# Order of weight loads, row gathers and a GpSimd power in the second layer's sorted expert tiles

## Chip, cores and metric

One core of a Trainium2 chip. The metric is the device time of one execution in microseconds; three runs of the kernel before gave 946.13, 953.25 and 954.22 (median 953.25). All arithmetic is fp32.

## The reference, cut to what matters

Two layers over 16 sequences of 112 tokens (1792 tokens of 256 values), each a gated cross-attention to 375 context rows and then a gated mixture of experts. The change sits in the second layer's experts:

```python
h_norm = layer_norm(h, rn_g, rn_b)
g = softmax(einsum('bsd,ed->bse', h_norm, router_w))        # 4 experts
top2_w, top2_idx = top_k(g, 2); top2_w /= sum(top2_w) + 1e-8
hid = relu(layer_norm(einsum('bsd,edh->bseh', h, w1), ln_g, ln_b))   # 256 -> 512
expert_out = einsum('bseh,ehd->bsed', hid, w2)                       # 512 -> 256
out = sum(expert_out[top2_idx] * top2_w)
return layer_norm(out, on_g, on_b)
```

## The kernel before

**Stages.** The first layer's attention and routed experts take up to 583 us; the rest of its experts follows, then the second layer's attention (its score matmuls run from 645 to 733 us). From 740 us on the second layer's experts run as 39 *units*, one in each step of the loop of L1519 (its index is j; unit j starts in step j). A unit is 128 rows through one expert:

- units 0 to 7: token tiles 0 and 1, each through all four experts ("dense");
- units 8 to 30: 23 *sorted tiles* (unit 8 + t is tile t). The middle ten token tiles are routed: each token goes to its two best experts only. Its two copies are gathered into tiles of 128 rows of one expert, with room for the worst case;
- units 31 to 38: token tiles 12 and 13, dense again. They keep TensorE busy while the tiles' results are gathered back.

**A unit's work**, spread over three steps: `unit_hidden` (L1323) multiplies by w1 into PSUM `ph` (4 matmuls, L1327) and takes the mean and variance on VectorE; `unit_normed` (L1337) makes the normed rows; one step later `unit_turn` (L1352) transposes them (`ptz`, L1356), and ScalarE applies scale, bias and relu (L1360); two steps later `unit_out` (L1366) multiplies by w2 into `py` (8 matmuls, L1371). A sorted tile's result is scaled on VectorE into `yr` (L1376) and stored to DRAM `yg1` by SyncE (L1377). A sorted tile's rows are transposed by `unit_in` (L1315, `px`, L1319) two steps before its unit.

**What feeds it.** The order of every engine's instructions in this part is the order of the program text (a manual schedule); each engine and the DMA-issuing queue of SyncE go through theirs in order. Three streams matter:

- *Weights.* `weights_in` (L1279) loads an expert's 1028 KB into one of six buffers, issued by SyncE (L1288; before it SyncE reads the expert's number into a register, L1284). Called at the end of step j for units up to j+3. The buffer that unit u takes was last read by unit u-6, whose last matmul is in step u-4. The store of unit u-5 is emitted earlier in the same step, so it stands ahead of the load of u in SyncE's queue.
- *Rows.* `rows_for` (L1303) issues a gather of 128 KB by GpSimd (L1307) into one of four buffers, at the end of step j for units up to j+4. A buffer is free again after the `px` of the unit four before.
- *Routing.* `routing()` (L1403) is a generator that is advanced by `go_on`, so many parts at a step as `counts` (L1506) says. It yields `taker` (L413), the list of rows that each tile gathers, and `of_rows` (L417).

**The later dense gates.** `dense_gates(R0 + NR, True)` (L1389) computes token tiles 12's and 13's weights in parts, advanced by `next(gating)` at L1541. It calls `gates_of`, whose VectorE differences (L270, L271) feed a power on GpSimd (L273) in place of an exponential on ScalarE. The results are read first in step 33.

**The end.** After the last tile's store, GpSimd gathers each routed token's two results (`fetch1`, L1454, 20 gathers), and `end_one` (L1447) adds, norms and stores a token tile. The number of `end_one` calls per step is listed at L1556. Every `fetch1` waits for all stores to `yg1`.

```python
            attended(n)
            beside(n, 1)
            go_on(counts.get(j, (0, 0))[1])
            if ahead + 4 <= j < stored:
                next(gating, None)
                if j % 3 == 0:
                    end_one()
            # then weights_in for units j+1 .. j+3, rows_for for units j+1 .. j+4
```

Here `ahead` is 8 and `stored` is 32.

Of the kernel before, what the change touches and what calls it, by code (L numbers as in the profile page):

```python
# [56 lines left out]
def tile_flamingo(  # L57
# [11 lines left out]
    def bc(ap, shape):  # L69
        return ap.unsqueeze(len(ap.shape)).to_broadcast(shape)  # L70
# [125 lines left out]
    def stats_of(mv, i, src):  # L196
        st = work.tile([P, 6], F32, tag="bnst", name="bnst")
        nc.vector.bn_stats(st, src)  # L198
        nc.vector.bn_aggr(mv[:, i, :], st)  # L199
# [62 lines left out]
    def gates_of(wk, lg, tops, e, nt, tiny, scale, powers=False):  # L262


        sh = [P, nt, e]
        n = nt * e
        both = wk.tile([P, n + nt], F32, tag=f"g{e}_{nt}", name="g", bufs=1)
        total = wk.tile([P, nt], F32, tag=f"gs{e}_{nt}", name="gs", bufs=1)
        g, second = both[:, :n].rearrange("p (i e) -> p i e", e=e), both[:, n:]
        nc.vector.tensor_tensor(g, lg, bc(tops[0], sh), ALU.subtract)  # L270
        nc.vector.tensor_sub(second, tops[1], tops[0])  # L271
        if powers:
            nc.gpsimd.tensor_tensor(both, euler.to_broadcast([P, n + nt]), both, ALU.pow)  # L273
        else:
            nc.scalar.activation(both, both, AF.Exp)
        yield
        nc.vector.tensor_reduce(total, g, AX.X, ALU.add)
        nc.vector.scalar_tensor_tensor(total, total, tiny, second, ALU.mult, ALU.add)
        nc.vector.tensor_scalar(total, total, 1.0, None, ALU.add)
        nc.vector.reciprocal(total, total)  # L280
        if scale is not None:
            nc.vector.tensor_scalar(total, total, scale, None, ALU.mult)
        gates = keep.tile([P, nt, 2], F32, tag=f"gates{e}_{nt}", name="gates")
        nc.vector.tensor_copy(gates[:, :, 0], total)
        nc.vector.tensor_mul(gates[:, :, 1], second, total)
        return gates
# [211 lines left out]
    with tc.tile_pool(name="a0", bufs=2) as a0, tc.tile_pool(  # L498
# [314 lines left out]
        def beside(n, where):  # L813
            place.update(at=where, n=0)
            for f, args in side.get((n, where), ()):
                f(*args)
# [22 lines left out]
    with tc.tile_pool(name="f0", bufs=3) as f0, tc.tile_pool(  # L839
# [69 lines left out]
        units = [(e, t0, w) for t0, w in blocks for e in range(ES)]  # L909
# [16 lines left out]
        at_i, owner_i, taker = (found[name] for name in ("at", "owner", "taker"))  # L926
# [23 lines left out]
    with tc.tile_pool(name="a1", bufs=2) as a1, tc.tile_pool(  # L950
# [315 lines left out]
        units = [(e, i) for e in range(E1) for i in dense_tiles[:R0]]  # L1266
        ahead = len(units)
        units += [(None, t) for t in range(TILES1)]
        units += [(e, i) for i in dense_tiles[R0:] for e in range(E1)]
        weights, loads = {}, []  # L1270

        def key_of(u):

            return ("t", u[1]) if u[0] is None else (units.index(u) < ahead, u[0])

        loads = [key_of(units[0]), key_of(units[R0])]
        routed = {}

        def weights_in(key):  # L1279
            w = wpool.tile([P, WR1], F32, tag="w", name="wr1_sb")  # L1280
            weights[key] = w
            kind, e = key
            if kind == "t":
                e = nc.values_load(  # L1284
                    routed["owner"][0:1, e : e + 1], engines=[mybir.EngineType.SP],
                    min_val=0, max_val=E1 - 1,
                )
                nc.sync.dma_start(out=w, in_=wr1[bass.ds(e, 1)].rearrange("o p w -> p (o w)"))  # L1288
            else:
                nc.sync.dma_start(out=w, in_=wr1[e])  # L1290
# [12 lines left out]
        def rows_for(u):  # L1303
            if u[0] is None and u not in asked:
                asked.add(u)
                g = ctx_pool.tile([P, KD, S], F32, tag="ctx", name="xg1_sb")[:, 0, :D]
                nc.gpsimd.indirect_dma_start(  # L1307
                    out=g, out_offset=None, in_=xn1_rows,
                    in_offset=bass.IndirectOffsetOnAxis(
                        ap=routed["taker"][:, u[1] : u[1] + 1], axis=0  # L1310
                    ),
                )
                rows_in[u] = g
# [9 lines left out]
        def unit_hidden(u):  # L1323
            w, x_u = weights[key_of(u)], xgs.pop(u) if u[0] is None else xrs[u[1]]
            ph = ps_mm.tile([P, HID], F32, tag="mm", name="ph1")
            for k in range(KD):
                nc.tensor.matmul(  # L1327
                    ph, x_u[:, k, :], w[:, k * HID : (k + 1) * HID],
                    start=(k == 0), stop=(k == KD - 1),
                )  # L1330
            mvh = f1.tile([P, 1, 2], F32, tag="mvh", name="mvh", bufs=4)
            stats_of(mvh, 0, ph)
            r = f1.tile([P, 2], F32, tag="rh", name="rh", bufs=4)
            nc.scalar.activation(r[:, 0:1], mvh[:, 0, 1:2], AF.Sqrt, bias=eps)
            hs[u] = ph, mvh, r
# [67 lines left out]
        def routing():  # L1403
            lg = lg1[:, R0 : R0 + NR, :]
            ohs, tops = yield from two_largest(f1, lg, E1, NR)
            parts = places(f1, ps_t, "t", ohs, E1, TILES1, NR)
            next(parts)
            yield
            gating = gates_of(f1, lg, tops, E1, NR, 1e-8, None)
            next(gating)  # L1410
            next(parts)
            yield
            routed["owner"] = next(parts)
            yield
            routed["at"] = at_once(parts)
            yield
            gates = at_once(gating)
            routed["taker"], routed["rows"] = yield from takers(
                f1, ps_t, "t", routed["at"], E1, TILES1, NR, gates,

                lambda: keep.tile([P, KD, N], F32, tag="oT", name="tables").rearrange(
                    "p k n -> p (k n)"
                ),
            )
# [50 lines left out]
        def attend(n):  # L1475
            if n < B:
                ps[n] = scores1(n)
            if n + 2 < B:
                context(n + 2)
                context_rows(n + 2)  # L1480
            if n == B - 2:
                for key in loads:
                    weights_in(key)
            if 0 <= n - 2 < B:
                apply1(n - 2, pTs.pop(n - 2))
            if n % G in (1, 2) and (n // G + 1) * G < B:
                queries1((n // G + 1) * G, n % G - 1)

        def attended(n):
            if n < B:  # L1490
                ps[n] = divided(*ps[n])
            if 0 <= n - 1 < B:
                pTs[n - 1] = turn1(ps.pop(n - 1))
# [9 lines left out]


        parts, gating = routing(), dense_gates(R0 + NR, True)
        counts = {1: (0, 2), 2: (1, 1), 3: (1, 2), 4: (1, 1), 5: (1, 1), 6: (1, 99)}  # L1506
        stored = ahead + TILES1 + 1
        fetches = [(R0, 0), (R0 + 1, 0)]
        for i in range(R0, R0 + NR):
# [5 lines left out]
        def go_on(k):  # L1515
            for _ in range(k):
                next(parts, None)

        for j in range(steps):  # L1519
            n = B + j  # L1520
            attend(n)
            if j < len(units):
                unit_hidden(units[j])
            beside(n, 0)
            if 0 <= j - 1 < len(units):
                unit_turn(units[j - 1])
            go_on(counts.get(j, (0, 0))[0])
            if j < len(units):
                unit_normed(units[j])
            if j >= ahead - 1:  # L1530
                first = j + 2 if j >= ahead else j + 1
                for u in units[first : j + 3]:
                    if u[0] is None:
                        unit_in(u)
            if 0 <= j - 2:
                unit_out(units[j - 2])
            attended(n)
            beside(n, 1)
            go_on(counts.get(j, (0, 0))[1])
            if ahead + 4 <= j < stored:  # L1540
                next(gating, None)  # L1541
                if j % 3 == 0:
                    end_one()

            for k in range(j + 1, min(j + 4, len(units))):
                if key_of(units[k]) not in weights and (units[k][0] is not None or "owner" in routed):
                    weights_in(key_of(units[k]))
            for k in range(j + 1, min(j + 5, len(units))):
                if "taker" in routed:
                    rows_for(units[k])  # L1550
            if j >= stored:
                for i, r in [fetches.pop(0) for _ in range(min(5 if j == stored else 4, len(fetches)))]:
                    fetch1(i, r)
                    if r:
                        to_end.append((i, ys[i, 0]))
                for _ in range((0, 0, 1, 1, 1, 2, 2, 2, 2)[j - stored]):  # L1556
                    end_one()
        while to_end or ending:
            end_one()
# [110 lines left out]
```

## Time and profile before

| what | us |
|---|---|
| runs | 946.13, 953.25, 954.22; median 953.25 |
| the profiled execution's own time | 950.83 |
| its span, first to last instruction | 949.1 |
| TensorE busy over the span | 880.1 (93%) |
| units 8 to 30, first `ph` of unit 8 to first `ph` of unit 31 | 791.15 to 897.21 = 106.06 |
| of that, TensorE busy | 98.94 |
| after the last sorted tile's store (908.6 to the end) | 40.4, TensorE busy 24.55 |

A profile line of the timeline reads: start, duration, engine, source line, operation, output<-inputs, shape, count, and in brackets the idle time before it with what ended it. SPq is SyncE's queue of DMA issues.

### The profile page before, as it was taken

Reading aid. Unit: us, or ns where it says so; the run is one execution under the profiler, and the core shown is the slowest. Engines: PE = TensorE matmul, PEld = TensorE weight load, DVE = VectorE, ACT = ScalarE, POOL = GpSimd, SP = SyncE. Lnnn points to the kernel's source line nnn. Section 1 sums busy time; section 2 is a strip of 40 time slices with the busy share of each in tenths; the row PEclk is TensorE's granted clock in tenths of the full one; section 3 lists DMA queues with packets and bytes.
Section 4 is the critical chain, followed back from the end, with each engine's and each line's share of the span. In section 5 each row is a group of like instructions: output and inputs, shape, how many; then the busy total and the mean of one; then the engine's idle time right before and its main releaser. Section 6 shows DMA issues by size and latency. Waiting matters only on the chain.

```text
span 949.1 us, 18431 instructions
## 1 busy us (share of the span) xinstructions
PE 880.1 (93%) x7168; PEld 637.6 (67%) x7168; DVE 473.4 (50%) x1253; ACT 349.8 (37%) x856; POOL 236.1 (25%) x439
## 2 busy tenths in 40 slices
PE   6899999999999979999999999989999898889994
PEld 3566666666666546789888887667778675656662
DVE  3666666565666435122222222675555554654557
ACT  3455555556555413101111110224222453444453
POOL 3231221110111120112222212771334303211054
PEclk9999999999999999799999999999999999999998
DMA  7300100010010001329999995422445243887844
GB/s 254 122 3 1 45 24 23 24 39 25 23 40 14 7 12 56 144 81 325 322 309 320 320 314 158 136 61 82 122 134 187 101 179 100 278 293 248 300 134 116
DMA packets 42871, 129.93 MB, mean 137 GB/s; under 512 B 5872, under 2 KB 22384, under 8 KB 33568
## 3 DMA queue, kind: packets, MB, share of 16 engines
q1 hardware_dynamic: 36384, 113.54, 35.6%
q0 software_dynamic: 5856, 14.69, 5.5%
q8 instruction: 56, 0.92, 0.4%
q10 hardware_dynamic: 544, 0.52, 0.2%
q14 instruction: 31, 0.25, 0.1%
HBM read 115.36 MB, written 13.37 MB: 136 GB/s over the span
## 4 chain that ended last, share of the span: by engine, by line
PE 73%; DMA 12%; DVE 7%; POOL 4%; issue 2%; ACT 2%; SPq 0%; DVEq 0%; POOLq 0%; ACTq 0%
DMA wr_sb<-in_wr_dram 10%; PE pt L638 6%; PE pt L657 6%; PE py L1371 5%; PE pt L537 5%; PE ph L1327 5%; PE sp L610 5%; PE phr L872 4%; PE ph L472 4%; PE pyr L884 4%; PE sp L550 3%; PE po L1170 3%; PE py L482 2%; PE ps L1121 2%; PE pa L1159 2%
## 5 line engine op out<-in xcount | busy, mean ns | idle before, releaser
L617 DVE TENSOR_REDUCE mz<-sp 112x2 f32<-112x750 f32 x128 | 114.2, 935 | 56.2 <-PE sp L610 56.2
L645 ACT ACTIVATE pT<-pt 125x336 f32<-125x336 f32 x256 | 94.7, 456 | 65.0 <-PE pt L638 65.0
L872 PE MATMUL phr<-xgT,wr_sb 128*128 128x128 f32 x656 | 82.9, 280 | 9.5 <-DVE xgT L862 9.2
L206 POOL TENSOR_SCALAR rstd<-mv 128x1 f32<-128x1 f32 (+1 forms) x49 | 12.4, 252 | 300.6 <-DVE mv L199 294.8
L872 PEld LDWEIGHTS phr<-xgT,wr_sb 128*128 128x128 f32 x656 | 77.2, 192 | 14.1 <-DVE xgT L862 13.9
L853 POOL DMA_INDIRECT xg_sb<-xn_rows,taker x41 | 39.1, 953 | 170.6 <-PE px L860 124.3
L877 ACT ACTIVATE hTr<-phr 128x512 f32<-128x512 f32 x41 | 24.5, 597 | 154.4 <-PE phr L872 154.4
L862 DVE TENSOR_SCALAR xgT<-px,wr_sb 128x128 f32<-128x128 f32 x82 | 24.9, 346 | 109.7 <-DMA wr_sb<-in_wr_dram 101.3
L884 PE MATMUL pyr<-wr_sb,hTr 128*128 128x256 f32 x328 | 77.4, 380 | 0.0
L1371 PE MATMUL py<-wr_sb,hT 128*128 128x256 f32 x312 | 77.4, 394 | 0.0
L657 PEld LDWEIGHTS pt<-pT,va 125*32 125x32 f32 x1536 | 38.0, 109 | 39.1 <-ACT pT L645 33.6
L884 PEld LDWEIGHTS pyr<-wr_sb,hTr 128*128 128x128 f32 x328 | 59.4, 191 | 6.3
L1371 PEld LDWEIGHTS py<-wr_sb,hT 128*128 128x128 f32 x312 | 58.4, 197 | 6.7
L638 PE MATMUL pt<-qm,kt 32*125 32x112 f32 x1536 | 61.2, 283 | 0.7 <-ACT kt L542 0.3
L657 PE MATMUL pt<-pT,va 125*32 125x112 f32 x1536 | 58.7, 264 | 2.0 <-ACT pT L645 2.0
L638 PEld LDWEIGHTS pt<-qm,kt 32*125 32x125 f32 x1536 | 49.1, 183 | 15.8 <-issue 11.7
L1360 ACT ACTIVATE hT<-ptz,wr_sb 128x128 f32<-128x128 f32 x156 | 57.9, 449 | 0.0
L610 PE MATMUL sp<-kt,qt 32*112 32x375 f32 x512 | 56.6, 494 | 1.2 <-ACT qt L569 0.8
L537 PE MATMUL pt<-ctx_sb,wk 128*128 128x375 f32 x128 | 51.6, 527 | 5.8 <-DMA ctx_sb<-in_ctxT_dram 5.8
L198 DVE BATCH_NORM_STATS2 bnst<-ph 128x6 f32<-128x512 f32 x39 | 27.2, 696 | 46.9 <-PE ph L1327 46.8
L1327 PE MATMUL ph<-wr_sb,xgT 128*128 128x512 f32 x92 | 46.3, 628 | 4.5 <-DMA wr_sb<-in_wr_dram 4.5
L542 ACT ACTIVATE kt<-pt,bks,spots 128x375 f32<-128x375 f32 x64 | 39.0, 659 | 22.7 <-PE pt L537 22.6
(273 smaller groups left out, 1520.3 us busy)
## 6 DMA issues: line engine op xcount, KB each, us to landing
wr_sb<-in_wr_dram SPq DMA_DIRECT2D x41, 1025.0 KB
wr_sb<-in_wr_dram SPq DMA_DIRECT2D x31, 1028.0 KB, 5.3
ctx_sb<-in_ctxT_dram SPq DMA_DIRECT2D x32, 375.0 KB, 5.7
yg<-yr SPq DMA_DIRECT2D x64, 128.0 KB, 6.7
ctxn_sb<-in_ctxN_dram SPq DMA_DIRECT2D x16, 375.0 KB
xn_rows<-xn SPq DMA_DIRECT2D x24, 128.0 KB, 2.5
out_dram<-yb SPq DMA_DIRECT2D x10, 128.0 KB, 1.7
w_sb<-in_w1s_dram SPq DMA_DIRECT2D x2, 512.0 KB
```

The lines of the kernel that those rows point to most:

```text
L537: nc.tensor.matmul(pk, wk0_sb[:, k, c * P : (c + 1) * P], ctxs[b][:, k, :], start=(k == 0), stop=(k == KD - 1),)
L610: nc.tensor.matmul(sps[j // 2][:TQ, j % 2, :S], qt[r : r + HP, c, t0 : t0 + TQ], kt[r : r + HP, g, u, :], start=True, stop=True,)
L617: nc.vector.tensor_reduce(mz[:, 2 * h : 2 * h + 2, HD * (1 - u)], sp[:TQ, :, :S], AX.X, ALU.max, negate=True,)
L638: nc.tensor.matmul(sts[j][:SC, s * TQ : (s + 1) * TQ], kt[r : r + HP, c // 2, c % 2, s * SC : (s + 1) * SC], qm[r : r + HP, :], start=True ...
L645: nc.scalar.activation(pT[:, j, :], sts[j][:SC, : NSC * TQ], AF.Exp)
L657: nc.tensor.matmul(po[r : r + HP, :], va[:, s, (c // 2) * 8 + j * 2 + c % 2, :], pT[:, j, s * TQ : (s + 1) * TQ], start=(s == 0), stop=(s ...
L853: nc.gpsimd.indirect_dma_start(out=g, out_offset=None, in_=xn_rows, in_offset=bass.IndirectOffsetOnAxis(ap=taker[:, t : t + 1], axis=0),)
L872: nc.tensor.matmul(ph[:, m, :], a[:, k, m * P : (m + 1) * P], xgT[:, k, :], start=(k == 0), stop=(k == KD - 1),)
L884: nc.tensor.matmul(py, hT[:, m, :], c[:, m, :], start=(m == 0), stop=(m == KH - 1))
L1327: nc.tensor.matmul(ph, x_u[:, k, :], w[:, k * HID : (k + 1) * HID], start=(k == 0), stop=(k == KD - 1),)
L1360: nc.scalar.activation(hT[:, m, :], pt[:, m, :], AF.Relu, bias=w[:, c + KH + m : c + KH + m + 1], scale=w[:, c + m : c + m + 1],)
L1371: nc.tensor.matmul(py, hT[:, m, :], w[:, c : c + D], start=(m == 0), stop=(m == KH - 1))
```

## The change

Four edits, all in the unit loop and in `gates_of`:

1. `weights_in` for units j+1 to j+3 is called after `unit_hidden` instead of at the end of the step: in SyncE's queue a load now stands ahead of the same step's store to `yg1`.
2. `rows_for` is called in the middle of the step, and for units up to j+5.
3. The last parts of `routing()` run in step 6 ahead of `unit_normed` (two parts there, none at the end of the step).
4. The dense gates' generator gets one more stop, between the differences and the power, and is advanced at j = 12, 13, 17 and 20 only; `end_one` takes the other multiples of 3 (15 to 30). In the last steps one `end_one` more is called at j = 36.

```diff
@@ gates_of
         nc.vector.tensor_sub(second, tops[1], tops[0])
         if powers:
+            yield
             nc.gpsimd.tensor_tensor(both, euler.to_broadcast([P, n + nt]), both, ALU.pow)
@@ the unit loop
-        counts = {1: (0, 2), 2: (1, 1), 3: (1, 2), 4: (1, 1), 5: (1, 1), 6: (1, 99)}
+        counts = {1: (0, 2), 2: (1, 1), 3: (1, 2), 4: (1, 1), 5: (1, 1), 6: (2, 0)}
...
             if j < len(units):
                 unit_hidden(units[j])
+
+            for u in units[j + 1 : j + 4]:
+                if key_of(u) not in weights and (u[0] is not None or "owner" in routed):
+                    weights_in(key_of(u))
             beside(n, 0)
             if 0 <= j - 1 < len(units):
                 unit_turn(units[j - 1])
             go_on(counts.get(j, (0, 0))[0])
+
+            if "taker" in routed:
+                for u in units[j + 1 : j + 6]:
+                    rows_for(u)
...
             if ahead + 4 <= j < stored:
-                next(gating, None)
-                if j % 3 == 0:
+
+                if j - ahead in (4, 5, 9, 12):
+                    next(gating, None)
+                elif j % 3 == 0:
                     end_one()
-
-            for k in range(j + 1, min(j + 4, len(units))):
-                if key_of(units[k]) not in weights and (units[k][0] is not None or "owner" in routed):
-                    weights_in(key_of(units[k]))
-            for k in range(j + 1, min(j + 5, len(units))):
-                if "taker" in routed:
-                    rows_for(units[k])
...
-                for _ in range((0, 0, 1, 1, 1, 2, 2, 2, 2)[j - stored]):
+                for _ in range((0, 0, 1, 1, 2, 2, 2, 2, 2)[j - stored]):
                     end_one()
```

Every engine gets the same instructions as before. TensorE's and ScalarE's are in the same order, but for three `end_one` square roots on ScalarE; SyncE's, GpSimd's and VectorE's change places as told.

## Prediction

> **What bounds the kernel now.** I read the page first: TensorE is busy 93% of the span, and the chain of work that ended last is 73% TensorE and 12% DMA. So time is lost where TensorE waits for DMA. The waits from 690 us on, where the changed loop runs, say which ones. Columns: who waited for whom, us in total, times, longest.
>
> ```profile
> POOL g L273 <- DVE g L271: 14.6, 1, 14.6
> ...
> PE px L1319 <- DMA xg_sb<-xn_rows,taker: 5.7, 3, 2.7
> ...
> PE ph L1327 <- DMA wr_sb<-in_wr_dram: 4.5, 2, 3.4
> ```
>
> TensorE waits three times for gathered rows and twice for weights. The first line is no loss by itself, but GpSimd is an in-order engine: what stands behind its power (L273) waits too. GpSimd's timeline:
>
> ```profile
> 783.53 1.09 POOL L1307 DMA_INDIRECT xg_sb<-xn_rows,taker  x1 [13.88 <-DVE of_rows L417]
> ...
> 802.90 0.94 POOL L1307 DMA_INDIRECT xg_sb<-xn_rows,taker  x1 [3.16 <-PE px L1319]
> 818.43 1.99 POOL L273 TENSOR_TENSOR g<-euler,g 128x10 f32<-128x10 f32 x1 [14.59 <-DVE g L271]
> 820.61 1.03 POOL L1307 DMA_INDIRECT xg_sb<-xn_rows,taker  x1 [0.19 <-issue]
> ```
>
> No gather is issued between 802.90 and 820.61, although one is due in every step. Next TensorE's timeline, the first `ph` matmuls of units 20, 21, 24 and 25:
>
> ```profile
> 845.64 1.88 PE L1327 MATMUL ph<-wr_sb,xgT 128*128 128x512 f32 x4
> ...
> 853.31 3.07 PE L1327 MATMUL ph<-wr_sb,xgT 128*128 128x512 f32 x4 [3.40 <-DMA wr_sb<-in_wr_dram]
> ...
> 867.40 1.88 PE L1327 MATMUL ph<-wr_sb,xgT 128*128 128x512 f32 x4
> 872.72 1.99 PE L1327 MATMUL ph<-wr_sb,xgT 128*128 128x512 f32 x4 [1.05 <-DMA wr_sb<-in_wr_dram]
> ```
>
> An undisturbed step is 4.10 us (`ph` at 837.44, 841.54, 845.64). The chain at unit 21 tells how late its load was:
>
> ```profile
> 844.40 8.87 DMA wr_sb<-in_wr_dram
> 853.26 0.04 issue
> 853.31 3.07 PE ph L1327 x4
> ```
>
> SyncE's queue tells why it began only at 844.40:
>
> ```profile
> 839.32 0.34 SPq L1288 DMA_DIRECT2D wr_sb<-in_wr_dram  x1
> 842.25 0.32 SPq L1377 DMA_DIRECT2D yg<-yr  x1
> 843.23 0.34 SPq L1445 DMA_DIRECT2D out_dram<-wv  x1
> 844.40 0.34 SPq L1288 DMA_DIRECT2D wr_sb<-in_wr_dram  x1
> ```
>
> The load of unit 21 stands behind the store of unit 16, which waits for that unit's `py` and VectorE. Its own buffer was free one step earlier. Last the stretches (length, busy of each engine, granted TensorE clock, DMA share, GB/s):
>
> ```profile
> 820.00:832.00 12.00, 9.34 (x34) 6.02 (x33) 6.85 (x23) 3.66 (x12) 5.23 (x6) 0.86 0.78 263
> 832.00:853.30 21.30, 17.91 (x79) 12.48 (x78) 11.82 (x27) 9.74 (x30) 4.72 (x5) 1.00 0.90 301
> 853.30:861.00 7.70, 7.69 (x23) 4.69 (x24) 2.34 (x5) 1.95 (x6) 0.94 (x1) 0.78 0.52 204
> ```
>
> After a stall the clock is 0.86 or 0.78: the `ph` group at 853.31 takes 3.07 us where others take 1.88. A stall costs its idle time and a slow stretch after it. The DMA engines are at 0.90 between stalls.
>
> **The change part by part.** TensorE's order does not change, so each stall can be costed by how late the next `ph` is against 4.10 us per step.
>
> *Routing's last parts earlier.* `taker` and `of_rows` are copied at 783.08 because they stand behind `wv` (L1383, 782.68), which waits for `py`. Their input, the `pn` matmuls, ends at 780.84. Moved ahead of the reciprocal they can run at about 780.9 (VectorE is done with the variance at 780.53), so the first gather starts some 2.3 us sooner. Before, TensorE waited 1.68 us for tile 0's rows and 1.33 us for tile 1's. The first landing (2.81 us after issue) then precedes TensorE's arrival at 784.80; the second gather, 1.4 us behind, lands at about 785.8 where TensorE arrives at 785.2: 0.6 us is left. The whole place costs: `ph` of unit 7 at 782.47 to unit 8 at 791.15 = 8.68, against 1.72+0.44+0.82+1.73 = 4.71 of work (two `px`), so 3.97; the next step 795.99-791.15 = 4.84, so 0.74; together 4.71. Saved: 4.71-0.6 = 4.1. What is pushed back is unit 6's reciprocal, 0.3 us; its reader on ScalarE starts only at 782.20, behind four relus, so this is free; uncovered it would cost 0.3.
>
> *Rows five ahead.* A gather is released by the `px` four units before, whatever its place in the text; only its place against the power counts. 0 by itself.
>
> *The power four units later.* It goes behind 15 gathers instead of 9. Its differences are still made in step 13, so at its new place (step 17) it waits for nothing; it takes 1.99 us between two gathers 4.10 us apart (0.94 busy, some 0.5 between instructions), which leaves about 0.7 us of cover. Uncovered it delays one gather by at most 2 us out of some 16 us of lead. Removed is the stall at 825.57 (2.66 idle): `ph` 820.60 to 828.30 = 7.70, to 833.34 = 5.04, so 3.60+0.94 = 4.54 saved. The gates are read in step 33, made in step 20.
>
> *Loads ahead of stores.* A load now follows the store of the step before, so from unit 14 on each is issued one step, 4.10 us, sooner. SyncE's register read before it (L1284) moves along. The load waits for a buffer whose last reader ended in step u-4, and the store behind it waits for a later `py` (step u-3): the store is not held up in the queue, but its bytes follow the load's. `yr` has four buffers, so 16 us of cover. With transfers as before, the two late loads (by 3.40 and 1.05) come 0.7 and 3 us early. Saved: at unit 21 (853.31-845.64)-4.10 = 3.57 and (859.20-853.31)-4.10 = 1.79; at unit 25 872.72-867.40-4.10 = 1.22 and 876.92-872.72-4.10 = 0.10. Together 6.7.
>
> *What comes after.* Without pauses the DMA engines get no time to catch up. A step needs 1028+128+128 KB = 1.315 MB; at the 301 GB/s of 832 to 853.3 that is 4.37 us, 0.27 more than the step. The load of unit 14 gets 816.49-806.08 = 10.4 us in place of 6.3; alone a load lands in 5.3 (median), so 5.1 us is spare; twelve steps with gathers eat 12×0.27 = 3.2 and leave 1.9. But one landing took 8.87, 3.6 over the median: I expect one or two short stalls, 2.0 us with their slow clock. Bounds: 0 (at 383 GB/s, the best slice of this region, a step takes 3.43) and 8 (at the 282 GB/s of 844 to 848: 4.66, twelve steps eat 6.7 of 5.1, and jitter with slow clock is on top).
>
> Two rules of the skill bear on this. First, "DMA: Bandwidth & Descriptors", section Specifications, gives some 358 GB/s of HBM per core: 3.67 us per step, the cover never shrinks, and the leftover stall would be 0. The row (301 at a share of 0.90, gathers and stores among the loads) says otherwise; I take the row, as it speaks against the change. Second, "TensorE: Matmul & The Clock Gate", section on HAM oscillation, sees the half clock after idle gaps of over about 3.4 us. By it only the stall of 3.40 costs more than its idle time, and the stalls before units 8 and 16 would save 2.4 and 2.7 instead of 4.1 and 4.5, 3.5 us less in all. The trace has a slow stretch after gaps of 1.68+1.33 and 2.66 as well (clock 0.86 over 820 to 832); I take the trace.
>
> *The end.* The fetches wait for the last store to `yg1`: issued at 905.69, landed 2.89 later, behind a load issued at 902.22. Other 128 KB stores land in 1.7. That load goes out a step sooner, so about 1.2 us is saved; 20 gathers, which GpSimd issues back to back, follow it. One more `end_one` at step 36 moves some 2 us of VectorE's work from after the last unit to before it. VectorE is nearly full from 926 to 946, so the sum stays: 0 (between -1 and +1.5).
>
> **The sum.** 4.1+4.5+6.7+1.2-2.0 = 14.5. The profiled execution took 950.83 (span 949.1): 936.3. The median of the runs shown is 2.4 above it: 938.7; I say 938.5.
>
> **The rivals.**
>
> *DMA-bound tiles (0.18).* The loads start sooner but do not end sooner, because the engines are full: at 4.66 us per step the late stalls come back, 6 to 10 us with slow clock. For it: shares of 0.9, landings of 7.5 and 8.87. Against it: after 878, without gathers, 302 GB/s carried steps of 3.9 us with no wait. Time: 943 to 948.
>
> *The end takes it back (0.07).* If the moved `end_one` meets a gather not yet landed, VectorE stalls in front of units 37 and 38 and each step slips by 2 to 3 us, and the first gather still comes late: 947 to 953. Against it: the gather concerned lands at 925.4, and its `end_one` would run at 925.4 at the earliest.
>
> *Slower (0.04).* One mechanism: continuous loads, stores and gathers slow each other, so that a step's bytes need over 5.25 us. From the load of unit 14 (about 804) to that of unit 30 before (its `ph` at 893.33) are 17 loads, 89 us: 5.25 each is break-even, 250 GB/s. At 5.6 the time is about 958. The slowest stretch between stalls was 282.
>
> *It doesn't do what it says (in the 0.07).* If a load were held by something other than the store, its issue would stay: against it, each load follows its store by 1.2 to 2.7 us, register read and an output's store between them.
>
> **How the numbers follow.** The likeliest, 938.5, has 0.71 and its own range 933 to 943. The range that should hold 8 in 10: low 931 (no leftover stall, end 1 us better, a run of the kind of 946), high 947 (most of the DMA-bound case). About 1% is what a measurement of this kernel can tell from no change. Under 943.7 lie the likeliest nearly whole and some of the DMA-bound case: 0.78; slower 0.04; the rest, 0.18, within 1%.
>
> **What would show it.** Right: first gather at about 781; no gather gap of over 5 us at 803 to 820; the power with hardly a wait behind the fifteenth gather; a load directly ahead of each tile's store; `ph` of unit 8 to 31 in about 95 us instead of 106.06. Wrong: `ph` waiting for `wr_sb` more than 3 us in all, landings growing beyond 10 us, or a longer stretch after the last tile's store than 40.4.

## The result, and the profile after

The changed kernel takes 943.62 us in the median of 22 runs (931.75 to 959.58), the kernel before 952.06 beside it (22 runs, 945.02 to 965.77). The ratio of the two is 0.9892, 95% interval 0.9864 to 0.992. That is 10.3 us less, somewhere between 7.6 and 12.9; foretold were 14.5, and 938.5 us. Some executions of either kernel run at a lower TensorE clock and take longer; the medians contain them, the ratio leaves them out. The profiled execution took 942.06 (span 940.4) against 950.83.

Cut at the first `ph` of a unit, the profiled executions compare as follows. The two columns on the right are runs told of below: the kernel before in a second trace, and the version that was found to be best.

| us | before | after | before_again | px_tail_back |
|---|---|---|---|---|
| start of unit 0 | 739.67 | 738.61 | 735.05 | 740.40 |
| unit 0 to 7 | 42.80 | 42.81 | 42.80 | 42.81 |
| unit 7 to 9 (first rows, routing) | 13.51 | 13.40 | 11.75 | 9.81 |
| unit 9 to 31 (sorted tiles) | 101.22 | 89.78 | 99.96 | 89.78 |
| unit 31 to the end | 51.91 | 55.76 | 54.74 | 50.74 |
| span | 949.1 | 940.4 | 944.3 | 933.5 |

Before against after: 1.06 come from ahead of the change and are chance (unit 0 starts between 735 and 744 whatever the kernel, in all traces but one), 0.1 from the place of the routing, 11.4 from the sorted tiles, and 3.9 are given back at the end. The tiles did what was foretold and more, the routing did nothing, and the end went the other way. Each has its own reason.

First TensorE's waits of the changed kernel from 690 us on (who waited for whom, us in total, times, longest):

```profile
PE ptz L1357 <- ACT hT L1350: 5.4, 2, 3.8
PE px L1320 <- ACT hT L1350: 3.1, 1, 3.1
...
PE ptz L1357 <- ACT hT L1361: 1.4, 1, 1.4
```

The lines that ended in DMA (`xg_sb` 5.7, `wr_sb` 4.5) are gone. But `px` waits 3.1 us for ScalarE, and `ptz` more than the 4.8 us of before: these are the routing and the end.

GpSimd's timeline (start, duration, instruction, idle time before it):

```profile
780.29 1.09 POOL L1308 DMA_INDIRECT xg_sb<-xn_rows,taker  x1 [11.69 <-DVE rh L1340]
...
826.33 0.95 POOL L1308 DMA_INDIRECT xg_sb<-xn_rows,taker  x1 [3.15 <-DVE bnst L198]
827.30 2.00 POOL L274 TENSOR_TENSOR g<-euler,g 128x10 f32<-128x10 f32 x1
830.45 1.03 POOL L1308 DMA_INDIRECT xg_sb<-xn_rows,taker  x1 [1.14 <-PE px L1320]
```

The first gather starts at 780.29 (before 783.53), and the power stands between two gathers without a wait of its own; before it had waited 14.59 us. The gather behind it is delayed by nothing that matters: idle time of 1.14 is left.

SyncE's queue around the load of unit 21, the one that was 3.40 us late:

```profile
829.51 0.33 SPq L1289 DMA_DIRECT2D wr_sb<-in_wr_dram  x1
832.44 0.33 SPq L1378 DMA_DIRECT2D yg<-yr  x1
833.61 0.33 SPq L1289 DMA_DIRECT2D wr_sb<-in_wr_dram  x1
```

and the `ph` of units 20 and 21 on TensorE:

```profile
839.93 1.88 PE L1328 MATMUL ph<-wr_sb,xgT 128*128 128x512 f32 x4
...
844.03 1.88 PE L1328 MATMUL ph<-wr_sb,xgT 128*128 128x512 f32 x4
```

The load of unit 21 is the one at 833.61: 6.3 us ahead of unit 20's `ph`, where it was 1.2 ahead (844.40 to 845.64). The last recorded signal of its landing is at 841.26, so 2.8 us are to spare, and unit 21 follows unit 20 after 4.10. A load still starts 1.2 us behind a store, but behind that of the step before.

Last the stretches (length, busy of PE, PEld, DVE, ACT, POOL, granted clock, DMA share, GB/s):

```profile
820.00:832.00 12.00, 12.00 (x55) 8.52 (x54) 7.23 (x18) 5.84 (x19) 4.92 (x4) 1.00 0.93 322
832.00:853.30 21.30, 21.30 (x93) 14.82 (x92) 15.39 (x43) 10.47 (x33) 4.73 (x5) 1.00 0.94 324
```

TensorE is busy without a gap at full clock, and the DMA engines carry 322 to 324 GB/s where they had carried 263 and 301. A step's 1.315 MB in 4.10 us is 321 GB/s: the engines keep up exactly.

### The profile page after: what moved, and what is told of

It is laid out like the page before. It is cut to its first block, busy times and chain, and to the rows that moved or that the text cites. A ratio compares the mean times of both kernels' runs of the same rounds, so it can differ in the third digit from the quotient of the medians.

```text
span 940.4 us, 18431 instructions
## 1 busy us (share of the span) xinstructions
PE 878.8 (93%) x7168; PEld 638.0 (68%) x7168; DVE 473.9 (50%) x1253; ACT 349.9 (37%) x856; POOL 235.9 (25%) x439
## 4 chain that ended last, share of the span: by engine, by line
PE 79%; DMA 7%; DVE 6%; POOL 3%; issue 2%; ACT 2%; another core or an unknown queue 0%; DVEq 0%; ACTq 0%; POOLq 0%
DMA wr_sb<-in_wr_dram 7%; PE py L1372 7%; PE ph L1328 6%; PE pt L639 6%; PE pt L658 6%; PE phr L873 5%; PE pt L538 5%; PE sp L611 5%; PE pyr L885 5%; PE ph L473 4%; PE sp L551 3%; PE po L1171 3%; PE py L483 2%; PE ps L1122 2%; PE pa L1160 2%
## 5 line engine op out<-in xcount | busy, mean ns | idle before, releaser
L639 PEld LDWEIGHTS pt<-qm,kt 32*125 32x125 f32 x1536 | 49.1, 183 | 15.7 <-issue 11.7
L473 PE MATMUL ph<-xT,w_sb 128*128 128x512 f32 (+1 forms) x112 | 46.4, 563 | 0.6 <-DVE x_sb L487 0.6
```

The costliest lines, as they stand in the source:

```text
L473: nc.tensor.matmul(ph, a[:, k, m * P : (m + 1) * P], xT[:, k, t0 * P : (t0 + n) * P], start=(k == 0), stop=(k == KD - 1),)
L639: nc.tensor.matmul(sts[j][:SC, s * TQ : (s + 1) * TQ], kt[r : r + HP, c // 2, c % 2, s * SC : (s + 1) * SC], qm[r : r + HP, :], start=True ...
```

## The experiments

Edits are against the changed kernel unless the text says otherwise. Ratios are to the kernel before on the same chip, with their 95% interval.

### The place of the routing

The first gather came 2.2 us sooner, counted from the start of unit 0 (41.68 us against 43.86), and still TensorE got from unit 7 to unit 9 only 0.1 sooner. TensorE's timeline of the changed kernel:

```profile
783.14 0.60 PE L1357 MATMUL ptz<-ident,hT 128*128 128x128 f32 x4
783.58 0.38 PE L1320 MATMUL px<-ident,xg_sb 128*128 128x128 f32 x2
787.02 0.44 PE L1320 MATMUL px<-ident,xg_sb 128*128 128x128 f32 x2 [3.06 <-ACT hT L1350]
...
789.92 2.68 PE L1328 MATMUL ph<-wr_sb,xgT 128*128 128x512 f32 x4
```

ScalarE's timeline of the same stretch:

```profile
784.35 0.29 ACT L1335 ACTIVATE rh<-mvh,eps 128x1 f32<-128x1 f32 x1 [2.42 <-DVE bnst L198]
784.55 1.49 ACT L1361 ACTIVATE hT<-ptz,wr_sb 128x128 f32<-128x128 f32 x4
785.92 0.79 ACT L1350 ACTIVATE hT<-ph,rh 128x512 f32<-128x512 f32 x1
786.58 0.38 ACT L1322 COPY xgT<-px 128x256 f32<-128x256 f32 x1
```

Tile 0's `px` runs without a wait at 783.58. Tile 1's comes right behind it in the program, but has to wait 3.06 us. `px` lives in a PSUM pool with one buffer, and this buffer is free only when ScalarE has copied it (L1322, 786.58 to 786.96). ScalarE comes to the copy behind a square root, four relus and unit 7's normed rows. Step 7 is the only step with two `px`. Before the change the rows were late by just about the same time, so the buffer was hidden behind them. Theory A: the buffer. Its rival: the gathers themselves.

*after_again*, the changed kernel a second time, as the base:

> The changed kernel once more, for its tail. In its first profile the stretch from the first ph of unit 31 to the end took 55.8 us (before: 51.9), with one odd pause of all engines near 906 to 913 us and two long waits of TensorE for the transposes of units 37 and 38 (3.81 and 1.64). If the moved end_one causes the loss, those two waits come back and the stretch is 54 to 56 us; if the odd pause causes it, the stretch is about 52 us in a profile without one.

944.12 us, ratio 0.99 (0.9867 to 0.9933). Unit 7 to 9 takes 11.70, the wait of 3.06 is there again, units 9 to 31 take 89.78, the end 54.93. (11.70 and not 13.40, as no stretch of half clock came behind the wait; see the last section.)

*no_routing*, the routing's last parts at the end of step 6 again:

```diff
-        counts = {1: (0, 2), 2: (1, 1), 3: (1, 2), 4: (1, 1), 5: (1, 1), 6: (2, 0)}
+        counts = {1: (0, 2), 2: (1, 1), 3: (1, 2), 4: (1, 1), 5: (1, 1), 6: (1, 99)}
```

> The changed kernel with the routing's last parts back at the end of step 6. By the prediction's term it loses about 4 us. By theory A (the wait for the PSUM buffer) it loses 0 to 0.5 us: the gathers start 2.3 us later, but tile 1's transpose could not start before unit 7's normed rows were made anyway.

943.87 us, ratio 0.9888 (0.9844 to 0.9931), against 944.12 on the same chip. Its intervals alone would hardly exclude 4 us, but its trace does: unit 7 to 9 takes 11.71, as in after_again. TensorE's timeline:

```profile
800.95 0.41 PE L1320 MATMUL px<-ident,xg_sb 128*128 128x128 f32 x2 [1.75 <-DMA xg_sb<-xn_rows,taker]
802.49 0.44 PE L1320 MATMUL px<-ident,xg_sb 128*128 128x128 f32 x2 [1.12 <-ACT xgT L1322]
```

With the rows late, tile 0 waits 1.75 for its rows and tile 1 another 1.12 for the buffer; with the rows early, tile 1 waits 3.06 for the buffer alone. (before_again shows the same pair, 1.72 and 1.22.) The edit by itself is worth nothing, and the 4.1 of the prediction are refuted.

*px_bank*, tile 1's `px` in the pool of `ph`, which has three buffers:

```diff
-            px = ps_t.tile([P, KD, P], F32, tag="t", name="px1")
+            if u[1] == 1:
+                px = ps_mm.tile([P, KD, P], F32, tag="mm", name="px1")
+            else:
+                px = ps_t.tile([P, KD, P], F32, tag="t", name="px1")
```

> The changed kernel with one edit: the transpose of tile 1's rows goes to a PSUM buffer of another pool. Theory A: the stall before unit 8 stayed (3.06 us) because tile 1's transpose needs the one PSUM buffer that tile 0's holds until ScalarE has copied it, and that copy stands behind unit 7's normed rows; then the stall falls to about 0.6 us, the slow clock after it goes too, and the time falls by about 4 us. Rival B: the rows themselves land late; then the wait stays near 3 us and moves to the gather, and the time stays.

942.22 us, ratio 0.9869 (0.983 to 0.9907). TensorE's timeline:

```profile
788.49 0.38 PE L1323 MATMUL px<-ident,xg_sb 128*128 128x128 f32 x2
789.29 0.44 PE L1323 MATMUL px<-ident,xg_sb 128*128 128x128 f32 x2 [0.43 <-DMA xg_sb<-xn_rows,taker]
...
791.94 1.98 PE L1331 MATMUL ph<-wr_sb,xgT 128*128 128x512 f32 x4 [0.48 <-issue]
```

The wait of 3.06 is gone, and what is left is the gather's 0.43: close to the 0.6 that the prediction had left for it. Unit 7 to 9 takes 9.80: 3.7 less than in the first trace of before, which had half clock behind its waits, and 1.9 less than in the second and in after_again, which had not. Theory A is shown: the earlier routing and the second buffer together are worth 1.9 us, or 3.7 where the half clock falls away too, of the 4.1 foretold, and the earlier routing alone nothing. The second buffer with the routing late was not run; tile 0's wait of 1.75 for its rows in no_routing is not one that it could remove. The times of px_bank and after_again alone (1.9 us apart) do not tell this; their traces do.

### The sorted tiles: loads, rows, power

*loads_back*, `weights_in` at the end of the step again:

> The changed kernel with the loads at the end of the step again, behind the stores. The prediction's term: units 9 to 31 take 89.8+6.7 = 96.5 us, and the time is 944.1+6.7 = 950.8. Theory E (the end is longer because the fetches start 1.2 us sooner after unit 31 and so meet the same units at another moment): the fetches start at +12.3 again and the end is back at 51.9, so the time is about 947. Theory F (the end doesn't hang on the loads): the end stays at 55 to 56, time 951.

```profile
PE ph L1328 <- DMA wr_sb<-in_wr_dram: 3.8, 4, 1.5
```

This line of TensorE's waits is back. Units 9 to 31 take 95.61, 5.8 more than with the loads ahead; 6.7 had been foretold. The time is 953.46, ratio 1.0015 (0.9967 to 1.0063). By the ratio this costs more than the trace shows (11.7 us against the changed kernel, or 7.1 at the lower end of the interval); the profiled execution, 951.43, is 7.3 and 9.4 above the two of the changed kernel; 1.6 of this lie in units 0 to 7, ahead of the tiles. The part beyond some 7 us is not explained.

The end does not become shorter, though the first fetch starts 12.94 us after unit 31 (before 12.31, in the changed kernel 11.10): 55.82. Theory E falls.

*power_back*, the power directly behind its differences, rows five ahead:

```diff
         if powers:
-            yield
...
-                if j - ahead in (4, 5, 9, 12):
+                if j - ahead in (4, 5, 9):
```

> The changed kernel with the power directly behind its differences again, rows still five ahead in the middle of the step. The prediction (rows five ahead are worth 0 by themselves, the power's place is worth 4.5): a gap of 2.7 us ahead of a px near unit 16 returns, units 9 to 31 take 94.3, time 948.6. Theory G (a gather placed five units ahead stands in front of the waiting power anyway, so either of the two edits would do): the power waits about 14 us with two gathers late behind it, no px waits, units 9 to 31 take 89.8, time 944.

GpSimd's timeline:

```profile
813.06 0.94 POOL L1307 DMA_INDIRECT xg_sb<-xn_rows,taker  x1 [3.16 <-PE px L1319]
820.31 1.99 POOL L273 TENSOR_TENSOR g<-euler,g 128x10 f32<-128x10 f32 x1 [6.30 <-DVE g L271]
822.50 1.03 POOL L1307 DMA_INDIRECT xg_sb<-xn_rows,taker  x1 [0.19 <-issue]
```

The power waits again (6.30 us, not the 14 that were expected), but two more gathers stand ahead of it (808.96 and 813.06), so the gathers behind it have time left. No `px` waits in the tiles, units 9 to 31 take 89.78 to the hundredth, 943.56 us, ratio 0.99 (0.987 to 0.993). Theory G holds, and the prediction's "0 by itself" for the rows is wrong as a statement about the edit: it would have done alone.

*rows_back*, the gathers four ahead at the end of the step, the power late:

> The changed kernel with the gathers four ahead at the end of the step again; the power stays four units behind its differences. The prediction (rows five ahead are worth 0 once the power is late) and theory G (either of the two edits takes the stall away) both say: no px waits near unit 16, units 9 to 31 take 89.8 us, time 943.6 to 944.1. Rival (the gathers' place in the step is what matters for the stall): the gap of 2.5 us and 94 us for units 9 to 31 stay, time 948.5.

No `px` waits there, units 9 to 31 take 89.78; 942.14 us, ratio 0.9936 (0.9909 to 0.9963) on a chip where the kernel before took 949.67. So the late power does it alone as well.

*rows_power_back*, both back:

> The changed kernel with both back: the power behind its differences, rows four ahead at the end of the step. By the prediction and by theory G alike the stall ahead of px near unit 16 returns: a gap of 2.7 us and a slow stretch, units 9 to 31 take 89.8+4.5 = 94.3, time 948.6. If no stall comes back, the stall of before hung on the loads instead, and the time is 944.

GpSimd's timeline:

```profile
813.68 1.99 POOL L273 TENSOR_TENSOR g<-euler,g 128x10 f32<-128x10 f32 x1 [14.50 <-DVE g L271]
815.87 1.03 POOL L1307 DMA_INDIRECT xg_sb<-xn_rows,taker  x1 [0.19 <-issue]
```

and TensorE's:

```profile
820.61 0.41 PE L1319 MATMUL px<-ident,xg_sb 128*128 128x128 f32 x2 [2.37 <-ACT hT L1360]
820.86 3.16 PE L1371 MATMUL py<-wr_sb,hT 128*128 128x256 f32 x8
```

The stall is back (the wait is put down to ScalarE, but the gather issued at 815.87 is what comes late: the last recorded signal of its landing is at 820.48, and ScalarE had copied the buffer before 817), with a slow `py` of 3.16 behind it in place of 1.89. Units 9 to 31 take 94.03, 948.49 us, ratio 0.9962 (0.9932 to 0.9991). The stall is worth 4.25, near the 4.54 foretold, and either of the two edits removes it.

Loads 5.8 and rows-or-power 4.25 are 10.1 together. Before's first trace gives 11.4, its second (99.96) 10.2: how late a load comes differs between executions.

### The end

*tail_back*, one `end_one` at step 36 as before:

```diff
-                for _ in range((0, 0, 1, 1, 2, 2, 2, 2, 2)[j - stored]):
+                for _ in range((0, 0, 1, 1, 1, 2, 2, 2, 2)[j - stored]):
```

> The changed kernel with one end_one instead of two at step 36, as before. Theory: the extra end_one stands in front of unit 37's statistics on VectorE, delays its transposes and leaves VectorE idle later; undone, the stretch from unit 31's first ph to the end falls to about 51 to 52 us and the time by 2 to 3 us. Rival: the sum of VectorE's work sets the end, so the place does not matter; then within 0.5 us.

945.04 us, ratio 0.9909 (0.9877 to 0.9941), the end 56.18 us; after_again, on the same chip, has 944.12 and 54.93. By this the second `end_one` costs nothing. The next runs show that an end cannot be compared so simply.

*before_again*, the kernel before for a second trace:

> The kernel before, unchanged, for a second trace of its end. Theory D (the change makes the end longer): from the first ph of unit 31 to the end it takes 51.9 us again (+-0.7), VectorE never waits for TensorE while TensorE has finished what it waits for, and the tiles (unit 8 to 31) take 106 with the three stalls. Rival (the first trace of before showed a good end, and the change has no part in it): the end takes 54.5 to 56 here too, with VectorE's waits of 1 to 2.6 us. Time by both: 951 to 955.

954.36 us, ratio 0.9995 (0.9963 to 1.0028), and the end takes 54.74, not 51.91. So two traces of one kernel differ by 2.8 us at the end, and of the 3.9 us given back a part has nothing to do with the change. What it is shows in the changed kernel's trace. VectorE's timeline:

```profile
908.50 0.70 DVE L198 BATCH_NORM_STATS2 bnst<-ph 128x6 f32<-128x512 f32 x1 [1.10 <-PE ptz L1357]
...
912.81 0.49 DVE L1384 SCALAR_TENSOR_TENSOR wo<-py,gates_d,wo 128x256 f32<-128x256 f32 x1 [2.56 <-remote]
```

The matmuls that they wait for, on TensorE:

```profile
904.01 1.88 PE L1328 MATMUL ph<-wr_sb,wq 128*128 128x512 f32 x4
...
907.18 1.89 PE L1372 MATMUL py<-wr_sb,hT 128*128 128x256 f32 x8
```

`ph` ends at 905.89, and VectorE takes it up at 908.50 after idling; `py` ends at 909.07, and `wo` starts at 912.81. TensorE's signals (by which it tells another engine that a result is there) arrive 2.6 and 3.7 us after the matmuls ("remote" is a sender that the profile does not name). The same traces lack some records of such signals (1143 to 1152 of TensorE's, 1160 in the others), also near 590 us, which the change does not touch. before, rows_back, px_again, px_between and px_tail_back have their signals on time; before_again, after and the other changed kernels have late ones. Where the chip is on record, the kind goes with the chip and not with the kernel: all traces from two chips are late (after_again, px_bank, tail_back and no_routing; before_again, loads_back, power_back and rows_power_back), all from two others on time. Whether the lateness also exists in executions that are not traced, or comes from the tracing, no run here tells. Only ends of the same kind are compared from here on: on time 51.91 before and 53.70 in rows_back; late 54.74 before and 54.5 to 55.8 for the changed order.

*px_again*, px_bank in more rounds:

> The changed kernel with tile 1's px in another PSUM pool, once more and in more rounds, as the base for the next. Theory A (one PSUM buffer under px): unit 7 to 8 takes 5.6 us instead of 7.6 to 8.5, so 2 to 3.5 us less than the changed kernel: ratio to before about 0.987. If the PSUM buffer only moves the wait, ratio 0.99.

939.63 us, ratio 0.9897 (0.9847 to 0.9946) on the chip of rows_back: 2.5 less than that. Unit 7 to 9 takes 9.81, the end 53.84 with signals on time.

*px_between*, from step 36 on one `end_one` ahead of the step's `wo`:

```diff
+            if j >= stored + 4:
+                end_one()
             if 0 <= j - 2:
                 unit_out(units[j - 2])
...
-                for _ in range((0, 0, 1, 1, 2, 2, 2, 2, 2)[j - stored]):
+                for _ in range((0, 0, 1, 1, 1, 1, 1, 1, 1)[j - stored]):
```

> The kernel of px_again, and from step 36 on one of the token tiles' ends (add, statistics, norm, store) comes ahead of the step's wo instead of behind it, in VectorE's order. Theory H (at the end VectorE is the bound, and its waits of 1.1 to 2.6 us for TensorE's late signals are holes that other ready work can fill): the hole ahead of wo in step 36 shrinks from 2.6 to under 1, the end from 55 to about 53.5, ratio about 0.985. Rival (what stands in the hole now delays the next unit's statistics by as much): the end stays at 55, ratio 0.987. If the moved end meets a gather that has not landed, it is longer: 57, ratio 0.989.

937.91 us, ratio 0.989 (0.9846 to 0.9935); the end is 52.34. It is 1.5 shorter by the trace, but not at the hole that was expected, which is not there with signals on time: the wait of the last but one `wo` for its `py` falls from 2.38 to 0.88. The times do not tell the two kernels apart.

*px_tail_back*, px_again with one `end_one` at step 36 (both diffs above):

> The kernel of px_again with one end_one at step 36 again, as before the change. Traces of the end fall in two kinds: with TensorE's signals on time (before 51.9 us from unit 31 to the end; rows_back 53.7, px_again 53.8, px_between 52.3) and with late ones (before_again 54.7; the changed kernels 54.5 to 55.8), and only like kinds are compared. Theory I (the second end_one in step 36 makes VectorE late for unit 37 and so TensorE late for its last transposes, 3.4 to 3.7 us at +37.8): with one, that wait is 2.7 or less and the end, in a trace with signals on time, is 51 to 52; ratio to before 1 to 3 us below that of px_again. Rival (the earlier fetches, not the end_one, moved the end): 53.5 or more with signals on time, ratio as px_again. In a trace with late signals: 54.5 to 56 by the rival, about 53.5 by theory I.

933.9 us, ratio 0.9794 (0.9745 to 0.9843), faster than both kernels. The end takes 50.74 with signals on time, 3.1 less than px_again. TensorE's last transposes in px_again:

```profile
914.86 0.66 PE L1360 MATMUL ptz<-ident,hT 128*128 128x128 f32 x4 [1.52 <-ACT hT L1353]
915.36 1.89 PE L1375 MATMUL py<-wr_sb,hT 128*128 128x256 f32 x8
920.99 1.12 PE L1360 MATMUL ptz<-ident,hT 128*128 128x128 f32 x4 [3.74 <-ACT hT L1353]
921.89 6.05 PE L1375 MATMUL py<-wr_sb,hT 128*128 128x256 f32 x16
```

and in px_tail_back:

```profile
913.13 0.66 PE L1360 MATMUL ptz<-ident,hT 128*128 128x128 f32 x4
913.62 1.89 PE L1375 MATMUL py<-wr_sb,hT 128*128 128x256 f32 x8
918.26 0.66 PE L1360 MATMUL ptz<-ident,hT 128*128 128x128 f32 x4 [2.74 <-ACT hT L1353]
918.75 3.62 PE L1375 MATMUL py<-wr_sb,hT 128*128 128x256 f32 x16
```

VectorE tells why. px_again:

```profile
911.45 0.69 DVE L198 BATCH_NORM_STATS2 bnst<-ph 128x6 f32<-128x512 f32 x1
...
916.06 0.43 DVE L198 BATCH_NORM_STATS2 bnst<-yb 128x6 f32<-128x256 f32 x1 [0.91 <-DMA yb<-yg,at_i]
...
925.55 0.48 DVE L1387 SCALAR_TENSOR_TENSOR wo<-py,gates_d,wo 128x256 f32<-128x256 f32 x1 [2.38 <-PE py L1375]
```

px_tail_back:

```profile
909.73 0.69 DVE L198 BATCH_NORM_STATS2 bnst<-ph 128x6 f32<-128x512 f32 x1
...
920.68 0.48 DVE L1387 SCALAR_TENSOR_TENSOR wo<-py,gates_d,wo 128x256 f32<-128x256 f32 x1 [0.21 <-PE py L1375]
```

With two `end_one` in step 36, VectorE takes the statistics of unit 37's `ph` 1.7 us later (911.45 against 909.73). The transposes of unit 37 wait 1.52, where they had not waited. VectorE then meets a gather that has not landed (0.91), and the last transposes wait 3.74 instead of 2.74. Around this longer wait the clock falls: it is 0.50 over 921 to 925, where px_tail_back has 1.00 over 918 to 922.5, and the last sixteen `py` take 6.05 us instead of 3.62. VectorE waits 2.38 us for them, and the end is VectorE's. In traces with signals on time, theory I is shown: the second `end_one` costs 3.1 us, by these steps. What it costs in executions that are not traced is not settled. By the ratios px_tail_back is 9.8 us below px_again, on another chip and more than the traces explain, while tail_back, on a chip whose traces have late signals, gained nothing by the same edit.

## Why the prediction was right, and where it was wrong

The direction was right, and 943.62 lies inside 931 to 947, just above the 933 to 943 of the likeliest case; the gain was 14.5 by the sum and is about 10 by the runs. The time alone would also fit the rival "DMA-bound tiles" (943 to 948). The trace refutes it: no `ph` waits for `wr_sb`, and the tiles gained 11.4 us where 4.5 + 6.7 - 2.0 = 9.2 were foretold. Term by term, with ends taken from traces with signals on time:

- **Rows five ahead and the power, 4.5.** Right as a pair: 4.25 in rows_power_back. Wrong as split: either of them would have done.
- **Loads ahead of stores, 6.7.** Right in kind, 5.8 measured by undoing it; the load of unit 21 now lands 2.8 us early, where 0.7 was foretold.
- **What comes after, -2.0.** Not there: 0. The step that failed is "the 301 GB/s of 832 to 853.3" taken as what the engines can carry. In the changed kernel the same engines carried 324 over the same stretch. The prediction had a counter-example at hand: the 302 GB/s after 878 are steps of 3.9 us without gathers, which ask for 303 and had no wait. So 302 there was what was asked for and not a limit. Why 832 to 853.3 carried only 301 stays open: it was not the stall itself, as 312 were carried in it (849.9 to 853.3). Of the two ways weighed there, the rule (cover does not shrink, stall 0) gave the right answer; its own figure is not reached in any run here.
- **Routing's last parts earlier, 4.1.** Mis-sized: 0 to 0.1. The step that failed is "the first landing then precedes TensorE's arrival at 784.80; the second gather lands at about 785.8": both are right (the first landing is recorded at 783.16, TensorE arrives at 783.58; in px_bank the second gather is 0.43 late where 0.6 was foretold), but the sum asked only when the rows arrive, not whether `px` has a place to go. The wait that took over (3.06 on ScalarE's copy) is as long as the two that went (1.68 and 1.33).
- **The end, +1.2 and 0.** The first fetch starts 1.2 us sooner, as foretold (11.10 us after unit 31 instead of 12.31), and the end is 1.2 shorter once the second `end_one` is taken away (50.74 against 51.91); that the fetches made it so was not tested alone. The `end_one`, "0 (between -1 and +1.5)", is -3.1 in these traces. The failed step is "VectorE is nearly full from 926 to 946, so the sum stays": VectorE's work does not only fill its own time, it also stands ahead of the statistics on which TensorE's next transposes hang. The rival "The end takes it back" told of part of this mechanism (a gather that has not landed, here 0.91) and dismissed it by the landing of one gather.

Together 0.1 + 4.25 + 5.8 + 0 + 1.2 - 3.1 = 8.3 by undoing each part, or 0.1 + 11.4 - 1.9 = 9.6 by before's first trace; the runs say 10.3 (7.6 to 12.9). That the time stayed inside the range is in part luck: the routing and the end were 4.0 and 3.1 too high, the loads 0.9, and the stall that did not come gave 2.0 back.

Of the signs named ahead, the first gather (780.29), the power behind its gathers, and 94.68 us for units 8 to 31 came as foretold. The sign "a longer stretch after the last tile's store than 40.4" had to be read with care: only against a trace of the same kind did it name a fault of the change.

## What to carry to other kernels

When a late input is moved earlier, look for the next thing that the waiting instruction needs: a single PSUM buffer whose reader stands in another engine's queue can hold exactly the time that was freed, and a second buffer in one step is the smaller edit. On an engine that TensorE waits for, work moved "from after to before" is not free because the total stays: ask what stands behind it in that engine's order. A rate measured in one stretch need not be what can be carried: compare it with what was asked for there. And a stage of one trace should be compared with a second trace of the same kernel before its cause is sought.

## What was not expected of the hardware

The same 3.06 us wait ahead of `px` cost 1.7 us more in some executions than in others: unit 7 to 9 took 13.39 or 13.40 in five traces that have this wait (after, tail_back, loads_back, power_back, rows_back), but 11.70 in after_again and rows_power_back. In the longer ones a stretch of half clock begins at or behind the wait (`ph` takes 2.68 us there; the clock is 0.72 over 787 to 793). In the record of the granted clock these stretches last 3.41 us, some twice or three times as long. The Trainium skill's "TensorE: Matmul & The Clock Gate", section "What's actually happening", tells of a free-running window of about 3.4 us that decides on the clock, so that the phase matters; the traces agree with the length, and with its being a matter of chance whether the wait is hit. They do not agree with the bound of 3.4 us on the gap that the prediction quoted: waits of 2.37 (rows_power_back) and 2.66 (before) were followed by slow stretches, while 2.74 at the end of px_tail_back was not.

TensorE's late signals (2.6 and 3.7 us after the matmuls' ends) were not foreseen either; they are told of above, and their cause stays open.
